# Two layers of attention and experts on one core: orders written by hand, set anew

## The chip, the cores and the metric

The kernel runs on one core of a Trainium2 chip, in float32. Its metric is the device time of one execution in microseconds (us). A core has five engines that run side by side, each through its own queue of instructions in order: TensorE (in the profile PE, with PEld for its weight loads), VectorE (DVE), ScalarE (ACT), GpSimd (POOL) and SyncE (SP), which here only starts DMA transfers. An engine waits on semaphores for the others. What is behind a waiting instruction in the same queue waits with it.

## The reference

```python
B, T, C = 4, 256, 1024                      # 1024 tokens of 1024 channels
x = x + lambda_layer(group_norm(x), ...)    # layer 0: q, k, v projections, content and position products
t = tokens(x)
t = t + attention(layer_norm(t), W_attn, b_attn, W_proj, b_proj)     # 16 heads, causal, 256 tokens
t = t + experts(layer_norm(t), gate_w, gate_b, expert_w, expert_b)   # 8 experts, kept where gate >= 0.1
```

The gate is a softmax over eight experts; weights below 0.1 are dropped and the rest are scaled to sum to one. Each expert is a 1024x1024 matrix.

## The kernel before

Tokens are worked on in eight tiles of 128 (`t`, `NT` = 8). Matrix products run in float32 as two passes, so a 128x128 by 128x512 product shows as two matmuls. Many products go by a scheme of seven block products instead of eight (`sums_of_A`, `sums_of_B` make the sums that it needs on VectorE). Accumulators lie in PSUM: three banks under the tag `mm`, three under `tr`, two under `sc`; a new user of a bank waits until the one three before it has been read out.

A list scheduler orders each engine's instructions by its own estimate of times, except within `tc.manual_schedule(...)`, where the engines named (all, if none is) keep the order in which the program is written. Two such sections that follow each other can still be merged: the first instructions of the later one can go ahead of the last of the earlier one.

**The end of layer 0 (L437 to L481).** Eight tiles, first the odd, then the even ones (`tiles`, position i). In each: `content` adds two products to `s0` (L375), two products `py` are added to the tile's rows in `x_at` (L477), and `layer_norm` (L183) takes statistics (L187 to L189), a square root on ScalarE (L132), and writes the normalised rows to one of three slots of `ln_rows` (L160). These rows are to be turned so that channels lie on the partitions: they go out to DRAM (L194), come back as four quarters (L173, `quarters_of`), and VectorE transposes 32x32 blocks of them into `ln1` (L178, `turn`). SyncE's order is the written one, that is, rows of tile i out, quarters of tile i in, rows of tile i+1 out; VectorE's order is the scheduler's. GpSimd adds a bias to the rows (L479) and stores them (L480). `project_v` then reads `ln1`: products 1 and 2 of the tiles in the order 1, 3, 0, 2, then product 3, then those that need `sums_of_B` (L507 to L510).

**Attention (L702 on).** 32 steps i, one pair of heads and one batch each. In step i VectorE turns the softmax rows of step i-3 (`turned`, L671), TensorE does some `project_qk` products (`units`), then `values` of step i-3 (L683), then `scores` of step i (L614); softmax follows on VectorE, ScalarE and GpSimd (`scored`), and its rows go out to DRAM and back on SyncE's queue (L662, L666). From step 22 on all engines keep the written order. From step 28 on, `project_out` of some token tile and half (t, j) stands in the step (`out_at`), its `values` after the seventh of its eight chunks. Half 0 uses `w_p0`, half 1 `w_p1`, which is loaded at step 28.

**Gating (L985 to L1110).** `project_out` of the remaining tiles is cut in chunks of one 128-row product (two matmuls). A counter `chunks` goes up by one per chunk, and the table `after` says at which count each of six stages of each tile's gate is written: 0 `normalise` (statistics, rows out, quarters in, residual rows to the output), 1 `turn_rows`, 2 `gate_sums` (L945), 3 `gate` (softmax, L953 to L972), 4 `place` (L979 to L1002), 5 `enter` (L1013). Tiles 6 and 7 are turned on TensorE (L931) from rows made on VectorE (L918). The first expert's two weight halves `w0` (2 MB each) and its bias are loaded on SyncE's queue ahead of this section.

**Experts (from L1275).** The last tile runs densely through expert 0 (`weighted`, L817), while its gate is finished; rows of the others are gathered by GpSimd (`get`, L802), transposed on VectorE (`put`, L178), multiplied (`products`, L1201) and added to the output by GpSimd (L825; the dense tile at L1296).

Of the kernel before, what the change touches and what calls it, by code (L numbers as in the profile page):

```python
# [32 lines left out]
F32 = mybir.dt.float32  # L33
# [6 lines left out]
P = 128  # L40
# [27 lines left out]
def kernel(  # L68
# [41 lines left out]
    def big_tile(n, name, shape=(NC, TOK)):  # L110
        return big[n].tile([P, *shape], F32, tag="big", name=name)

    def w_tile(name, *parts, home=None):

        w = (home or wpool).tile([P, NC, HALF], F32, tag="w", name=name)
        at = 0
        for part in parts:
            n = part.shape[1]
            nc.sync.dma_start(w[:, :, at : at + n], part.rearrange("(c p) n -> p c n", p=P))
            at += n  # L120
        return w

# [43 lines left out]
        )  # L166
        return done

    def quarters_of(rows, home, name):

        row = home.tile([P, Q, C // Q], F32, tag="xg", name=name)
        for f in range(Q):
            nc.sync.dma_start(row[ts(f, 32), :, :], rows[:, f, :].rearrange("(g j) c -> j g c", j=32))  # L173
        return row
# [5 lines left out]
            row[:, : slots // 32, :].rearrange("p g (c i) -> p g c i", c=NC),  # L180
        )

    def layer_norm(ln, t, dst, home, turns):  # L183

        stats = small.tile([P, 2, 6], F32, tag="ln_stats", name=f"ln1_stats{t}")
        for j in range(2):
            nc.vector.bn_stats(stats[:, j, :], xs[t][:, ts(j, HALF)])  # L187
        mv = small.tile([P, 2], F32, tag="ln_mv", name=f"ln1_mv{t}")
        nc.vector.bn_aggr(mv, stats)  # L189
        rstd = small.tile([P, 1], F32, tag="ln_rstd", name=f"ln1_rstd{t}")  # L190
        inverse_root(rstd, mv[:, 1:2], EPS)
        done = normalised(ln, xs[t], mv[:, 0:1], rstd)
        rows = turns.tile([P, Q, C // Q], F32, tag="rows", name=f"ln1_rows{t}")
        nc.sync.dma_start(rows.rearrange("n f c -> n (f c)"), ln)  # L194
        turn(dst[:, :, ts(t, P)], quarters_of(rows, home, f"ln1_quarters{t}"))
        return done


    with ExitStack() as layer0:
# [254 lines left out]
        turns = layer0.enter_context(tc.tile_pool(name="turns0", bufs=3, space=bass.MemoryType.DRAM))  # L454
        ln_rows = wpool.tile([P, 4, C], F32, tag="w", name="ln_rows")
        bp = ln_rows[:, 3, :]
        nc.gpsimd.dma_start(bp, b_proj.partition_broadcast(P))
        with tc.manual_schedule(engines={mybir.EngineType.SP}):
            for i, (b, nt) in enumerate(tiles):
                if i == 0:  # L460
                    content(b, nt)
                if i + 1 < NT:
                    content(*tiles[i + 1])
                t = 2 * b + nt
                for hp in range(2):
                    py = mm(f"py{t}_{hp}")
                    for hl in range(2):
                        bh = b * HEADS0 + 2 * hp + hl
                        for mh in range(2):
# [14 lines left out]
    with ExitStack() as attention:  # L484
# [41 lines left out]
        def project_v(r):  # L526
            a = [w_v[r][:, 4 * j : 4 * j + 4, ts(i, M)] for i in range(2) for j in range(2)]
            a11, a12, s3, a22 = a
            s1, s2, s4 = (s_v[:, r, i, :, :] for i in range(3))
            with tc.issue_after(ln_done.ins):  # L530
                sums_of_A(*a, s1, s2, s4)

            def one(t, n, a, b):
                return product(f"pv{r}_{t}_{n}", lambda c: b[:, c, ts(t, P)], lambda c: a[:, c, :], M)

            def homes(t):
                return [v1[2 * r + i][:, 4 * l + t, :] for i in range(2) for l in range(2)]

            in_time = (1, 3, 0, 2)
            for t in in_time:  # L540
                c11, c12, c21, c22 = homes(t)
                nc.scalar.copy(c22, one(t, 1, a11, b11))
                nc.vector.tensor_add(c11, one(t, 2, a12, b21), c22)
            if r == 0:
                sums_of_B()

            for t in in_time:
                nc.scalar.copy(homes(t)[1], one(t, 3, s4, b22))
            for t in range(4):
# [170 lines left out]
        for i in range(written):  # L720
# [8 lines left out]


        units = {
            22: ([(6, 4), (6, 5)], []),
            23: ([], [(7, 1)]),
            24: ([(7, 2)], [(7, 6)]),
            25: ([(7, 7), (7, 4)], []),
            26: ([(6, 3)], [(7, 5)]),
            27: ([(7, 3)], []),
        }
        out_at = {28: (0, 0), 29: (1, 0), 30: (0, 1), 31: (1, 1), 32: (2, 0), 33: (2, 1)}
        with tc.manual_schedule():  # L740
            for i in range(written, len(steps) + lag):
                if i == written:
# [43 lines left out]
    weights = ExitStack()  # L786
    w_even, t_pool = pool(weights, "w_even", 2), pool(weights, "t_pool")

    def half_weights(e, r, home, name="w_e"):

        return w_tile(f"{name}{e}_{r}", expert_w[e][:, ts(r, HALF)], home=home)
# [67 lines left out]
    with ExitStack() as gating:  # L859
# [40 lines left out]
        nc.vector.memset(kept, 0.0)  # L900
        kept_short = l2.tile([P, 2], F32, tag="kept_short", name="kept_short")

        def normalise(t):

            stats = small.tile([P, 2, 6], F32, tag="ln_stats", name=f"ln2_stats{t}")
            for j in range(2):
                nc.vector.bn_stats(stats[:, j, :], xs[t][:, ts(j, HALF)])  # L907
            mv = small.tile([P, 2], F32, tag="ln_mv", name=f"ln2_mv{t}")
            nc.vector.bn_aggr(mv, stats)
            rstd = small.tile([P, 1], F32, tag="ln_rstd", name=f"ln2_rstd{t}")  # L910
            inverse_root(rstd, mv[:, 1:2], EPS)
            row = l2w.tile([P, C], F32, tag="ye", name=f"row{t}", bufs=3)
            if t < NT - 2:
                normalised(row, xs[t], mv[:, 0:1], rstd)
                nc.sync.dma_start(rows[ts(t, P), :], row)
                row = quarters_of(rows[ts(t, P), :].rearrange("n (f c) -> n f c", f=Q), l2w, f"quarters{t}")
            else:
                nc.vector.tensor_scalar(row, xs[t], mv[:, 0:1], rstd, ALU.subtract, ALU.mult)  # L918
            nc.sync.dma_start(out[ts(t, P), :], xs[t])
            return row  # L920

# [132 lines left out]
                nc.vector.tensor_copy(slot[ts(g, 32), a:b, :, :], pc[ts(g, 32), a:b, :, g::Q])  # L1054
# [8 lines left out]
        def stage(n, t):  # L1063
# [24 lines left out]

        def one_more():
            nonlocal chunks  # L1090
            chunks += 1
            for t in after:
                for n, at in enumerate(after[t]):
                    if at == chunks:
                        stage(n, t)

        with tc.manual_schedule():
            for t in range(3, NT):
                for j in range(2):
# [34 lines left out]
        w, bias, step, T, T3, A, S = {0: w0}, {0: bias0}, {}, {}, {}, {}, {}  # L1134

        def load(e):
            w[e] = [half_weights(e, r, w_odd if e % 2 else w_even) for r in range(2)]
# [137 lines left out]
        with tc.manual_schedule():  # L1275
# [3 lines left out]
            for k in range(3):  # L1279
# [2 lines left out]
                lambda: gated[NT - 1][0][:, 0, 1:2],  # L1282
                turned_rows[NT - 1],
                w0,
                bias0,
                l2w,
                "dense",
                {
# [144 lines left out]
```

## Time and profile before

| what | value |
|---|---|
| runs shown | 1303.72, 1301.97, 1301.44 us |
| median | 1301.97 us |
| profiled execution: its own time | 1300.31 us |
| profiled execution: span from first to last instruction | 1298.5 us |
| mean granted TensorE clock | 0.984 |
| busy: PE, DVE, POOL, ACT | 1245.8, 709.9, 358.0, 214.7 us |

The profile comes from one execution. In a timeline a line has the start, the time, the engine, the source line, the operation with output<-input, the count, and in brackets the idle time of that engine before it and what ended it. "issue" is a wait that the profile can't ascribe. Busy time of TensorE is not time at full rate: after a long wait its instructions take about twice as long for some us.

### The profile page before, as it was taken

To read this page: it belongs to the slowest core of one execution; us is meant where nothing else is said; L and a number is where in the kernel's file an instruction comes from. 1 tells how busy PE (TensorE), PEld (TensorE's weight loads), DVE (VectorE), ACT (ScalarE), POOL (GpSimd) and SP (SyncE) were. 2 spreads that over 40 slices of the span, in tenths; PEclk is the share of its full clock that TensorE was granted. 3 is DMA by queue.
4 is the path that set the end of the run, shared out by engine and by line. 5 is a ranking of instruction groups with operands and counts; after the bars stand their busy time and mean duration, and the time that the engine had idled before them with its cause. 6 is when DMAs were issued, how large, how long until landed. Compare 5 with 4: busy or idle time off the path is not lost.

```text
span 1298.5 us, 12774 instructions
## 1 busy us (share of the span) xinstructions
PE 1245.8 (96%) x4562; PEld 650.9 (50%) x4562; DVE 709.9 (55%) x1303; ACT 214.7 (17%) x502; POOL 358.0 (28%) x439
## 2 busy tenths in 40 slices
PE   9999999978999999998988799899999999999998
PEld 5444894767884444443433344444344434443443
DVE  5884210686333666655544565756657464665642
ACT  3300111110000222222122223101111011011110
POOL 0000160250000222221221011543644554263530
PEclk9999999999999999998989899999999999999999
DMA  9020022854202535352377524455667475647442
GB/s 351 4 65 14 3 71 67 316 182 143 65 1 65 154 107 162 100 172 85 101 232 220 179 98 141 151 146 134 159 184 223 98 218 139 174 106 219 97 81 51
DMA packets 92823, 171.31 MB, mean 132 GB/s; under 512 B 9392, under 2 KB 47296, under 8 KB 92752
## 3 DMA queue, kind: packets, MB, share of 16 engines
q1 hardware_dynamic: 77616, 122.64, 28.7%
q0 software_dynamic: 15136, 47.78, 15.6%
q8 instruction: 38, 0.62, 0.2%
q14 instruction: 33, 0.27, 0.1%
HBM read 116.64 MB, written 49.55 MB: 128 GB/s over the span
## 4 chain that ended last, share of the span: by engine, by line
PE 42%; DVE 3%; issue 2%; DMA 2%; POOL 1%; ACT 1%; SPq 0%; DVEq 0%; POOLq 0%; ACTq 0%
PE p L1201 29%; PE po L701 6%; PE left L1243 3%; PE rest L1257 2%; PE last_pe L1358 1%; DMA w_p<-in_W_projT_dram 1%; DMA w_e_xg<-rows,gather 1%; POOL w_e_xg L802 1%; PE pqk L519 1%; PE pa L683 1%; DVE ln_stats L907 0%; DVE row_T L178 0%; PE sc L614 0%; PE parts L945 0%; POOL out_dram L1296 0%
## 5 line engine op out<-in xcount | busy, mean ns | idle before, releaser
L802 POOL DMA_INDIRECT w_e_xg<-rows,gather x146 | 155.1, 1062 | 61.5 <-issue 41.1
L1201 PE MATMUL p<-w_e,A 128*128 128x512 f32 x368 | 165.4, 600 | 1.6 <-DVE slot L1054 1.6
L656 POOL TENSOR_TENSOR s_q<-s_q,total 128x128 f32<-128x128 f32 (+1 forms) x128 | 64.4, 533 | 330.7 <-DVE total L653 330.7
L701 PE MATMUL po<-w_p,y_T 128*128 128x512 f32 x256 | 122.5, 619 | 5.8 <-DMA w_p<-in_W_projT_dram 5.8
L1201 PEld LDWEIGHTS p<-w_e,A 128*128 128x128 f32 x368 | 70.4, 192 | 91.6 <-issue 90.6
L1201 PE MATMUL p<-T,S 128*128 128x512 f32 x256 | 112.7, 592 | 0.0
L825 POOL DMA_INDIRECT out_dram<-y,add x32 | 57.4, 1794 | 178.1 <-ACT y L1207 116.7
L1207 ACT ACTIVATE y<-y,slot 128x512 f32<-128x512 f32 x64 | 46.0, 721 | 344.0 <-DVE y L1215 187.5
L284 PE MATMUL pq<-w_q,xn 128*128 128x512 f32 x224 | 99.6, 596 | 1.4 <-DVE q_s L288 1.1
L642 ACT ACTIVATE s_q<-s,top 128x256 f32<-128x256 f32 (+1 forms) x128 | 56.6, 443 | 194.7 <-issue 151.5
L519 PE MATMUL pqk<-ln,w_qk 128*128 128x512 f32 x192 | 86.9, 603 | 0.0
L1201 PEld LDWEIGHTS p<-T,S 128*128 128x128 f32 x256 | 48.6, 190 | 60.8 <-issue 60.5
L701 PEld LDWEIGHTS po<-w_p,y_T 128*128 128x128 f32 x256 | 46.9, 195 | 54.7 <-issue 46.7
L178 DVE STREAM_TRANSPOSE A<-w_e_xg 128x1024 f32<-128x1024 f32 x32 | 39.6, 1238 | 56.6 <-DMA w_e_xg<-rows,gather 56.6
L284 PEld LDWEIGHTS pq<-w_q,xn 128*128 128x128 f32 x224 | 41.8, 190 | 51.8 <-issue 47.3
L519 PEld LDWEIGHTS pqk<-ln,w_qk 128*128 128x128 f32 x192 | 36.5, 193 | 44.3 <-issue 43.4
L519 PE MATMUL pqk<-T,S_qk 128*128 128x512 f32 x128 | 58.4, 599 | 0.0
L1201 PE MATMUL p<-T,A 128*128 128x512 f32 x128 | 57.5, 592 | 0.0
L1201 PE MATMUL p<-w_e,S 128*128 128x512 f32 x128 | 57.5, 592 | 0.0
L519 PE MATMUL pv<-w_v,ln 128*128 128x256 f32 x192 | 45.7, 393 | 10.0 <-DVE ln L178 10.0
L519 PEld LDWEIGHTS pv<-w_v,ln 128*128 128x128 f32 x192 | 37.8, 198 | 16.2 <-issue 10.7
L1243 PE MATMUL left<-w_e,one 128*32 128x512 f32 x312 | 41.8, 593 | 0.0
(268 smaller groups left out, 1751.3 us busy)
## 6 DMA issues: line engine op xcount, KB each, us to landing
w_e<-in_expert_w_dram SPq DMA_DIRECT2D x16, 2048.0 KB, 12.4
s_rows<-s_q SPq DMA_DIRECT2D x32, 384.0 KB, 2.4
s_rows<-s_rows SPq DMA_DIRECT2D x128, 96.0 KB, 2.3
w_qk<-in_W_attnT_dram SPq DMA_DIRECT2D x8, 1024.0 KB, 6.1
xn<-in_xT_dram SPq DMA_DIRECT2D x8, 512.0 KB, 7.8
x_at<-in_x_dram SPq DMA_DIRECT2D x8, 512.0 KB, 7.4
w_v<-in_W_attnT_dram SPq DMA_DIRECT2D x2, 2048.0 KB, 12.6
ln_rows<-ln_rows SPq DMA_DIRECT2D x8, 512.0 KB, 4.6
```

The lines of the kernel that those rows point to most:

```text
L178: nc.vector.transpose(row_T[:, :, :slots].rearrange("p c (g j) -> p g c j", j=32), row[:, : slots // 32, :].rearrange("p g (c i) -> p g c ...
L284: nc.tensor.matmul(pq, xn[:, c, ts(t, P)], w_q[kc][:, c, :], start=(c == 0), stop=(c == NC - 1))
L519: nc.tensor.matmul(bank, stationary(c), moving(c), start=(c == 0), stop=(c == NC // 2 - 1))
L642: nc.scalar.activation(blocks(h, qt), s[:, h, cols].rearrange("p (b f i) -> p b f i", f=Q, i=32), AF.Exp, bias=top[:, qt, h : h + 1], accu ...
L656: nc.gpsimd.tensor_mul(blocks(h, qt), blocks(h, qt), total[:, qt, h : h + 1].unsqueeze(2).unsqueeze(3).to_broadcast([P, 1 + qt, Q, 32]),)
L701: nc.tensor.matmul(po, y_T[:, c, ts(t, P)], w_p[j][:, c, :], start=(c == 0), stop=(c == NC - 1))
L802: nc.gpsimd.indirect_dma_start(out=row[:, g, :], out_offset=None, in_=table[: (TOK - P) * Q, :] if e in SHORT else table, in_offset=bass.I ...
L825: nc.gpsimd.indirect_dma_start(out=out[: TOK - P, :] if e in SHORT else out, out_offset=bass.IndirectOffsetOnAxis(ap=add[:slots, e, k : k ...
L1201: nc.tensor.matmul(bank, a[:, c, :], b[:, c, :], start=(c == 0), stop=(c == NC // 2 - 1))
L1207: nc.scalar.mul(y[i][:, ts(j, HALF)], y[i][:, ts(j, HALF)], slot[:, e, 1, 2 * pair + i : 2 * pair + i + 1])
L1243: nc.tensor.matmul(bank[ts(i, 32), :], stationary, w[of][j][:, c, :], start=(c == 0), stop=(c == NC - 1))
L1257: nc.tensor.matmul(bank[ts(i, 64), :], A[e, last][:, i * (NC // 2) + c, :64], w[e][j][:, i * (NC // 2) + c, :], start=(c == 0), stop=(c == ...
```

## The change

In layer 0, `turn` is taken out of `layer_norm` and VectorE's order is the written one: the turn of the tile at position i-1 stands after the normalisation of the tile at position i, for positions 0 to 5. The last two turns stand after the first `sums_of_A` of `project_v`; the quarters of these two tiles land in slots of `ln_rows`. In attention, one product moves from step 22 to 23, and `out_at` has another order and a seventh entry, so that the gating section begins with the second half of tile 3. In gating, the table `after` is new; the first expert's weights and bias are written at chunks 14, 20 and 26, the weights on GpSimd's queue; two instructions that load a function table into ScalarE are added; half the statistics of the last tile are written earlier, its rows are made in two halves, and seven warming matmuls are left out. In the experts, the fourth gather stands ahead of the dense tile's addition to the output.

```diff
-    def w_tile(name, *parts, home=None):
+    def w_tile(name, *parts, home=None, queue=nc.sync):
...
-            nc.sync.dma_start(w[:, :, at : at + n], part.rearrange("(c p) n -> p c n", p=P))
+            queue.dma_start(w[:, :, at : at + n], part.rearrange("(c p) n -> p c n", p=P))
...
-    def layer_norm(ln, t, dst, home, turns):
+    def layer_norm(ln, t, quarters, turns):
...
-        turn(dst[:, :, ts(t, P)], quarters_of(rows, home, f"ln1_quarters{t}"))
+        quarters_of(rows, quarters)
...
+        def turn_ln(t):
+            turn(ln1[:, :, ts(t, P)], to_turn[t])
...
-        with tc.manual_schedule(engines={mybir.EngineType.SP}):
+        with tc.manual_schedule(engines={mybir.EngineType.SP, mybir.EngineType.DVE}):
...
-                ln_done = layer_norm(ln_rows[:, i % 3, :], t, ln1, tpool, turns)
+                if i < NT - 2:
+                    to_turn[t] = tpool.tile([P, Q, C // Q], F32, tag="xg", name=f"ln1_quarters{t}")
+                else:
+                    to_turn[t] = ln_rows[:, NT - 1 - i, :].rearrange("p (f c) -> p f c", f=Q)
+                ln_done = layer_norm(ln_rows[:, 2 if i == NT - 1 else i % 3, :], t, to_turn[t], turns)
+                if 0 < i < NT - 1:
+                    turn_ln(tiles[i - 1][0] * 2 + tiles[i - 1][1])
...
-            with tc.issue_after(ln_done.ins):
+            if r == 0:
+                with tc.manual_schedule(engines={mybir.EngineType.DVE}):
+                    with tc.issue_after(ln_done.ins):
+                        sums_of_A(*a, s1, s2, s4)
+                    for b, nt in tiles[-2:]:
+                        turn_ln(2 * b + nt)
+            else:
                 sums_of_A(*a, s1, s2, s4)
...
-            22: ([(6, 4), (6, 5)], []),
-            23: ([], [(7, 1)]),
+            22: ([(6, 4)], []),
+            23: ([(6, 5)], [(7, 1)]),
...
-        out_at = {28: (0, 0), 29: (1, 0), 30: (0, 1), 31: (1, 1), 32: (2, 0), 33: (2, 1)}
+        out_at = {28: (0, 0), 29: (1, 0), 30: (2, 0), 31: (0, 1), 32: (1, 1), 33: (2, 1), 34: (3, 0)}
...
+        def first_stats(t):
+            half_stats[t] = small.tile([P, 2, 6], F32, tag="ln_stats", name=f"ln2_stats{t}")
+            nc.vector.bn_stats(half_stats[t][:, 0, :], xs[t][:, :HALF])
...
-                nc.vector.tensor_scalar(row, xs[t], mv[:, 0:1], rstd, ALU.subtract, ALU.mult)
+                for j in range(2):
+                    half = slice(j * HALF, j * HALF + HALF)
+                    nc.vector.tensor_scalar(row[:, half], xs[t][:, half], mv[:, 0:1], rstd, ALU.subtract, ALU.mult)
...
-        w0 = [half_weights(0, r, w_even) for r in range(2)]
-        bias0 = expert_bias(0, l2w)
+        w0, bias0 = [], []
...
-            0: (1, 11, 13, 14, 19, 24),
-            1: (3, 20, 22, 23, 28, 33),
-            2: (12, 29, 31, 32, 37, 42),
-            3: (21, 38, 40, 41, 46, 51),
-            4: (33, 47, 49, 50, 55, 60),
-            5: (49, 59, 61, 62, 67, 72),
-            6: (65, 69, 71, 72, 76, 79),
+            0: (8, 13, 16, 17, 22, 27),
+            1: (8, 21, 24, 25, 30, 35),
+            2: (14, 29, 32, 33, 38, 43),
+            3: (22, 37, 40, 41, 46, 51),
+            4: (33, 45, 48, 49, 54, 59),
+            5: (49, 58, 61, 62, 67, 72),
+            6: (65, 69, 71, 72, 76, 80),
...
+        def load_table(function):
+            of = small.tile([P, 1], F32, tag="first", name="first", bufs=1)
+            nc.scalar.activation(of, ident[:, 0:1], function)
+        others = {
+            14: lambda: w0.append(half_weights(0, 0, w_even, queue=nc.gpsimd)),
+            20: lambda: w0.append(half_weights(0, 1, w_even, queue=nc.gpsimd)),
+            26: lambda: bias0.append(expert_bias(0, l2w)),
+            74: lambda: load_table(AF.Sqrt),
+            77: lambda: first_stats(NT - 1),
         }
...
+            chunks = NC - 1
+            one_more()
             for t in range(3, NT):
-                for j in range(2):
+                for j in range(t == 3, 2):
...
-            for _ in range(14):
+            for _ in range(7):
                 nc.tensor.matmul(warm[:, :P], before, ones, start=True, stop=True)
             stage(0, NT - 1)
+            load_table(AF.Exp)
...
+            get(0, 3)
             nc.gpsimd.indirect_dma_start(
...
-            get(0, 3)
             for e in range(E):
```

More of the change, by code (lines that the diff above doesn't have):

```diff
@@ L167, in normalised, with quarters_of @@
         return done
-    def quarters_of(rows, home, name):
-        row = home.tile([P, Q, C // Q], F32, tag="xg", name=name)
+    def quarters_of(rows, row):
         for f in range(Q):
@@ L456 @@
         bp = ln_rows[:, 3, :]
+        to_turn = {}
+        def turn_ln(t):
+            turn(ln1[:, :, ts(t, P)], to_turn[t])
         nc.gpsimd.dma_start(bp, b_proj.partition_broadcast(P))
-        with tc.manual_schedule(engines={mybir.EngineType.SP}):
+        with tc.manual_schedule(engines={mybir.EngineType.SP, mybir.EngineType.DVE}):
             for i, (b, nt) in enumerate(tiles):
@@ L787, with half_weights @@
     w_even, t_pool = pool(weights, "w_even", 2), pool(weights, "t_pool")
-    def half_weights(e, r, home, name="w_e"):
-        return w_tile(f"{name}{e}_{r}", expert_w[e][:, ts(r, HALF)], home=home)
+    def half_weights(e, r, home, name="w_e", queue=nc.sync):
+        return w_tile(f"{name}{e}_{r}", expert_w[e][:, ts(r, HALF)], home=home, queue=queue)
     def expert_bias(e, home, name="w_e", tag="bias", bufs=1):
@@ L901 @@
         kept_short = l2.tile([P, 2], F32, tag="kept_short", name="kept_short")
+        half_stats = {}
+        def first_stats(t):
+            half_stats[t] = small.tile([P, 2, 6], F32, tag="ln_stats", name=f"ln2_stats{t}")
+            nc.vector.bn_stats(half_stats[t][:, 0, :], xs[t][:, :HALF])
         def normalise(t):
-            stats = small.tile([P, 2, 6], F32, tag="ln_stats", name=f"ln2_stats{t}")
-            for j in range(2):
-                nc.vector.bn_stats(stats[:, j, :], xs[t][:, ts(j, HALF)])
+            if t not in half_stats:
+                first_stats(t)
+            stats = half_stats[t]
+            nc.vector.bn_stats(stats[:, 1, :], xs[t][:, HALF:])
             mv = small.tile([P, 2], F32, tag="ln_mv", name=f"ln2_mv{t}")
@@ L915, in normalise @@
                 nc.sync.dma_start(rows[ts(t, P), :], row)
-                row = quarters_of(rows[ts(t, P), :].rearrange("n (f c) -> n f c", f=Q), l2w, f"quarters{t}")
-            else:
-                nc.vector.tensor_scalar(row, xs[t], mv[:, 0:1], rstd, ALU.subtract, ALU.mult)
+                row = l2w.tile([P, Q, C // Q], F32, tag="xg", name=f"quarters{t}")
+                quarters_of(rows[ts(t, P), :].rearrange("n (f c) -> n f c", f=Q), row)
+            else:
+                for j in range(2):
+                    half = slice(j * HALF, j * HALF + HALF)
+                    nc.vector.tensor_scalar(row[:, half], xs[t][:, half], mv[:, 0:1], rstd, ALU.subtract, ALU.mult)
             nc.sync.dma_start(out[ts(t, P), :], xs[t])
@@ L1078 @@
         after = {
-            0: (1, 11, 13, 14, 19, 24),
-            1: (3, 20, 22, 23, 28, 33),
-            2: (12, 29, 31, 32, 37, 42),
-            3: (21, 38, 40, 41, 46, 51),
-            4: (33, 47, 49, 50, 55, 60),
-            5: (49, 59, 61, 62, 67, 72),
-            6: (65, 69, 71, 72, 76, 79),
+            0: (8, 13, 16, 17, 22, 27),
[5 more added lines that the diff above has]
+            6: (65, 69, 71, 72, 76, 80),
+        }
+        def load_table(function):
[7 more added lines that the diff above has]
+            77: lambda: first_stats(NT - 1),
         }
@@ L1095, in one_more @@
                         stage(n, t)
+            others.get(chunks, lambda: None)()
         with tc.manual_schedule():
+            chunks = NC - 1
+            one_more()
             for t in range(3, NT):
-                for j in range(2):
+                for j in range(t == 3, 2):
                     project_out(t, j, {c: one_more for c in range(NC)})
@@ L1133 @@
         w_odd, two = pool(pairs, "w_odd", 2, side="right"), pool(pairs, "two", 2, side="right")
-        w, bias, step, T, T3, A, S = {0: w0}, {0: bias0}, {}, {}, {}, {}, {}
+        w, bias, step, T, T3, A, S = {0: w0}, {0: bias0[0]}, {}, {}, {}, {}, {}
         def load(e):
@@ L1284 @@
                 w0,
-                bias0,
+                bias0[0],
                 l2w,
```

## The prediction

> **What bounds the kernel now.** I read the page first, then the waits of TensorE, then its timeline round each wait, then the queues behind them.
>
> ```profile
> span 1298.5 us, 12774 instructions
> PE 1245.8 (96%) x4562; PEld 650.9 (50%) x4562; DVE 709.9 (55%) x1303; ACT 214.7 (17%) x502; POOL 358.0 (28%) x439
> ```
>
> TensorE is busy for all but 52.7 us, so only those, and stretches where it works slowly, can be won. The waits of TensorE (releaser; total, times, longest) say where they lie:
>
> ```profile
> PE pv L519 <- DVE ln L178: 10.0, 2, 8.1
> PE pa L683 <- DVE s_T L671: 8.5, 3, 5.8
> PE parts L945 <- issue: 7.7, 1, 7.7
> PE po L701 <- DMA w_p<-in_W_projT_dram: 5.8, 1, 5.8
> PE pn L1123 <- DVE U L1213: 2.8, 1, 2.8
> PE parts L945 <- DVE row_T L178: 2.4, 4, 0.8
> PE p L1201 <- DVE slot L1054: 1.6, 1, 1.6
> ```
>
> Every one is touched. TensorE's timeline shows that a long wait costs twice:
>
> ```profile
> 278.06 7.07 PE L519 MATMUL pv<-w_v,ln 128*128 128x256 f32 x32
> 293.28 5.80 PE L519 MATMUL pv<-w_v,ln 128*128 128x256 f32 x16 [8.15 <-DVE ln L178]
> 300.91 3.69 PE L519 MATMUL pv<-w_v,ln 128*128 128x256 f32 x16 [1.83 <-DVE ln L178]
> 599.02 1.55 PE L683 MATMUL pa<-s_T,v 128*64 128x256 f32 x8 [5.76 <-DVE s_T L671]
> 662.99 7.85 PE L701 MATMUL po<-w_p,y_T 128*128 128x512 f32 x14 [5.79 <-DMA w_p<-in_W_projT_dram]
> 699.67 0.87 PE L683 MATMUL pa<-s_T,v 128*64 128x256 f32 x8 [1.67 <-DVE s_T L671]
> 719.64 1.08 PE L945 MATMUL parts<-row_T,gw 128*32 128x128 f32 x16 [7.74 <-issue]
> 846.06 5.88 PE L1201 MATMUL p<-w_e,A 128*128 128x512 f32 x8 [1.62 <-DVE slot L1054]
> ```
>
> Sixteen `pv` take 5.80 after 8.15 us of waiting, 3.69 after 1.83. From 846 on the chain of waits is TensorE alone to the last two products, so what is won earlier comes through to the end.
>
> **The change, part by part.** Times are those of the profiled execution.
>
> *Layer 0: turns in written order.* VectorE's timeline around the first turns:
>
> ```profile
> 242.42 0.16 DVE L159 SCALAR_TENSOR_TENSOR ln_less<-ln_mv,ln_rstd 128x1 f32<-128x1 f32 x1
> 255.43 1.25 DVE L178 STREAM_TRANSPOSE ln<-ln_quarters 128x1024 f32<-128x1024 f32 x1
> 289.31 1.23 DVE L178 STREAM_TRANSPOSE ln<-ln_quarters 128x1024 f32<-128x1024 f32 x1
> ```
>
> The scheduler turned too late: tile 3's quarters landed at 270.7, its turn came at 289.31, and the quarter buffer it held kept SyncE back. That goes. But the new place is early. Turn 0 follows position 1's normalisation, which ends at 242.6; its quarters landed at 251.8. VectorE now stands still for 9.2 us, and behind it are the adds that free TensorE's banks. After a turn VectorE needs four adds of 0.69, two statistics of 0.69, five small steps and ScalarE's root: 5.3 us to the next normalisation's end. From one such end to that tile's turn: 1.5 (ScalarE's rows), 4.6 (rows landing, median), 4.6 (quarters, first issue to last landing) and 1.2 for the turn. So two tiles take 1.5+4.6+4.6+1.2+5.3 = 17.2 us where TensorE's pace is 2x7.0. Chain of ends: position 2 at 258.4, 3 at 265.1, then 4 at 275.6, 5 at 282.3, 6 at 292.8; turn 5 ends 294.3, position 7 ends 298.2 (before: 283.5). Rows 6 land at 298.9, SyncE issues their quarters until 300.8, rows 7 land at 305.4, their quarters at 310.1, turn 7 ends at 311.4. Before it ended at 307.4, with TensorE waiting on the sums right behind it (0.76 us). So +4. Bounds: with the shortest landings of this stretch (3.6 and 4.4) turn 7 ends about 307.5, +0; with long ones (5.2 and 5.3) about 317.5, +10. I take the medians.
>
> TensorE waits about 4 us twice in that loop; rows show no slowing after 1.83 and slowing after 5.76, nothing between. [...]
>
> The next weight half is loaded when `ln_rows` is free, now after turn 7 (311) and not at 303.4. Its first user starts at 340, its sums at 317 with 3.6 us to spare; 0 to +2, I take 0.
>
> *Product (6,5) from step 22 to 23.* Before, step 23's `values` had nothing in front and waited 5.76 for a turn written behind `sums_qk` on VectorE; with slow products after it, 584.47 to 610.46 took 26.0 us. New: TensorE reaches the end of step 22 at 589.7 and of (6,5) at 593.2. VectorE: mask 0.96 and maxima 1.0 to 591.9, sums 2.7 to 594.6, reciprocal and turn to 595.7. Wait 2.5, too short for slowing. Work 17.45 + 2.5 = 19.95: -6.0 (bounds -6.5, -3 if it slows).
>
> *Steps 28 to 34.* `w_p1` landed at 662.95; TensorE wanted it at 657. With (2,0) in between it is wanted 8.7 us later, at 665.7: a margin of 2.7. Turn 28 is the tightest: quarters landed 669.9, wanted turned at 671.9. Step 34 gets work before its `values`, so the 1.67 goes. TensorE's work alone from 656.08 to the eighth chunk adds up to 698.0, against 707.5: -9.5 (bound -6).
>
> *Gating.* The 7.74 is SyncE's queue:
>
> ```profile
> 701.15 0.40 SPq L119 DMA_DIRECT2D w_e<-in_expert_w_dram  x1
> 701.63 0.74 SPq L795 DMA_DIRECT2D w_e_bias<-in_expert_b_dram  x1
> 702.43 1.80 SPq L915 DMA_DIRECT2D rows<-row  x1
> ```
>
> Tile 0's rows were normalised at 687.3, were issued at 702.43 behind a weight half that waited for memory, and landed at 713.8 behind 4 MB. Without these three ahead they go at once. Tiles 0 to 2 are complete 7 to 22 us before their chunks; the wait goes with about 1.5 of slowing. Three chunks instead of two between turn and `gate_sums` remove 2.4, the list waits (1.02, 0.64, 0.33) go. GpSimd pays two issues at about 0.9 each (the gate weights' issue in as many pieces took 0.91), with nothing waiting behind. At the end of the section the root's table load (1.28), one statistic (0.6) and half a scaling (0.4) leave the path; the warming products were not on it.
>
> Against this stands one new wait. At chunk 49 the table now names tile 4's softmax ahead of tile 5's normalisation, both at 49; before, the softmax came at 50. It holds VectorE for 2.8 to 3.8 us (744.71 to 747.51, 722.99 to 726.76). Tile 5's rows had no slack: turned at 776.97, wanted at 777.18. So about 3.5 us of new wait before its `gate_sums`; with smaller ones in a denser VectorE I take 6. Net -(7.74+1.5+2.4+2.0+2.3)+6 = -10 (bounds -15, -6).
>
> ScalarE's rows show 1.28 for a table load and the next instruction 0.01 us later. [...]
>
> *Expert 0.* The fourth gather stood behind the output add, which waited until 830.74; VectorE then stood 4.56 us for it, with the bank readers behind. Now its four issues (1.26 each) start when turn 0 frees a buffer at 821.8, end at 828 and leave the add its time. VectorE is at the list copies' end by 842.0 instead of 846.16, TensorE goes on at 842.3 instead of 846.06, without the slow products (5.88 for eight against 3.6): -6.0; the earlier exponential table takes 0.4. I take -5.8 (bound -3).
>
> Sum: 4 - 6.0 - 9.5 - 10 - 5.8 = -27.3. From the profiled 1300.31: 1273.0. The median stands 1.66 above that execution: **1275**.
>
> **Rivals.** *Slower:* layer 0's in-order turns eat it all. Price by the same chain: 8 tiles at the loop's longest landings (7.84 and 5.56) put turn 7 at 331, +24, total 1295; it decides against the change from a round trip of 16 us on (+36, 1307). For it: the first round trip took 13.4. Against: that one ran beside 6 MB of loads; the later ones took 8 to 10. Chance 0.11. *Between:* that chain at 1290 to 1300, 0.06.
>
> *Weights start early.* The chunk numbers order GpSimd's queue but delay nothing, and the first half's memory is free once (7,3) is done, at 638. `w_p0` shows such a start: 559.63, for a step that began at 584. Then 2 MB (8.0 us alone) run beside `w_p1` and the softmax rows: up to 5 us of wait for `w_p1`, +1 to 2 slow: 1282. Chance 0.18.
>
> *All cover holds:* quiet landings in layer 0 (+0), no new gating wait: 1265. Chance 0.17. *No effect* would need layer 0 to lose just what the rest wins: 0.03 for within 0.2%, about what a measurement here can tell from no change. Forecast: 0.45.
>
> **Numbers.** The likeliest is 1275. Far ends of the terms: 0-6.5-9.5-15-6.5 gives 1264; +10-3-6-6-3 gives 1294, and part of the slower-leaning cases adds 2. Faster 0.86, same 0.03, slower 0.11.
>
> **What would show it.** Right: in layer 0 waits of about 4 us on VectorE's adds in the loop and turn 7 near 311; `w_p` and `issue` gone from TensorE's waits; `parts` waiting 3 to 5 us once, for tile 5; `pn` gone. Wrong: turn 7 beyond 320 (layer 0), or a wait on `w_p` at 665 (early weights).

## The result, and the profile after

The kernel after takes 1284.93 us (median of four runs, 1284.55 to 1286.41) against 1302.85 for the kernel before, run beside it (1301.44 to 1303.81): ratio 0.9865, 95% interval 0.9848 to 0.9883. The forecast was 1275. The profiled execution took 1284.55, its span is 15.8 us shorter than that of before. The page:

```profile
span 1282.7 us, 12735 instructions
...
PE 1238.7 (97%) x4548; PEld 646.4 (50%) x4548; DVE 707.5 (55%) x1305; ACT 212.9 (17%) x502; POOL 361.9 (28%) x441
```

TensorE now stands idle for 44.0 us (1282.7 less 1238.7) instead of 52.7, and its own time fell by 7.1: seven warming products are gone, and fewer products follow a long wait (the mean granted clock is 0.992 instead of 0.984). Its waits (total, times, longest):

```profile
PE parts L972 <- issue: 11.8, 1, 11.8
PE pv L530 <- DVE s_v L152: 3.9, 1, 3.9
PE parts L972 <- DVE row_T L177: 3.2, 1, 3.2
PE pa L700 <- DVE s_T L688: 3.2, 2, 2.1
PE pc L366 <- DVE s L374: 3.1, 2, 2.1
PE py L474 <- DVE s L374: 2.2, 1, 2.2
```

`w_p`, `pn` and `ln` are gone from this view. The `issue` wait, which was to go, has grown from 7.7 to 11.8. TensorE's timeline at the places that the prediction named:

```profile
595.07 0.95 PE L700 MATMUL pa<-s_T,v 128*64 128x256 f32 x8 [2.08 <-DVE s_T L688]
...
597.53 7.92 PE L530 MATMUL pqk<-ln,w_qk 128*128 128x512 f32 x16
...
766.71 1.08 PE L972 MATMUL parts<-row_T,gw 128*32 128x128 f32 x16 [3.25 <-DVE row_T L177]
...
831.97 3.67 PE L1244 MATMUL p<-w_e,A 128*128 128x512 f32 x8 [1.32 <-DVE slot L1081]
```

Step 23 waits 2.08, tile 5's gate sums 3.25, and the products behind the list copies (`slot`) only 1.32. What stands behind the 11.8 is seen where all engines are listed together, from the last `values` product on:

```profile
692.15 1.24 ACT L160 ACTIVATE row<-xb,ln_less,ln_rstd 128x1024 f32<-128x1024 f32 x1 [18.45 <-PE pa L700]
...
693.41 0.34 SPq L939 DMA_DIRECT2D rows<-row  x1
...
694.25 0.93 POOL L119 DMA_DIRECT2D w_e<-in_expert_w_dram  x1
...
695.41 0.90 POOL L119 DMA_DIRECT2D w_e<-in_expert_w_dram  x1
...
696.65 1.93 SPq L172 DMA_DIRECT2D quarters<-rows  x4
...
711.83 1.08 PE L972 MATMUL parts<-row_T,gw 128*32 128x128 f32 x16 [11.81 <-issue]
...
714.14 1.74 SPq L172 DMA_DIRECT2D quarters<-rows  x4
```

ScalarE could write tile 0's row only at 692.15, after standing 18.45 us; its wait ended with the last `values`. SyncE sent the row at 693.41 and asked for the quarters at 696.65. In between GpSimd issued both weight halves, at 694.25 and 695.41, and the quarters landed at 704.32 to 710.36, 13.7 us from the first issue to the last landing; those of tile 3, later and with no weights beside them, took 4.4 (728.33 to 732.68). Tile 1's row, issued at 699.15, landed at 714.12.

By the prediction's own terms, from the two traces:

| term | predicted | traces |
|---|---|---|
| layer 0 | +4 | 65.6 (246.66 to 312.26) to 65.8 (246.01 to 311.79): +0.2 here; +2.5 alone (run below) |
| step 22 to 23 | -6.0 | 26.0 to 21.4: -4.6 |
| steps 28 to 34 | -9.5 | 51.45 to 41.9: -9.5 |
| gating, to the dense products | -10 | 98.7 to 102.1: +3.4 |
| expert 0 | -5.8 | 39.9 to 37.0, and 8 products 5.9 to 3.7: -5.1 |
| sum | -27.3 | -15.6 |

### The profile page after: what moved, and what is told of

Its sections match the earlier page's. It is cut to its first block, busy times and chain, and to the rows that moved or that the text cites. A ratio compares the mean times of both kernels' runs of the same rounds, so it can differ in the third digit from the quotient of the medians.

```text
span 1282.7 us, 12735 instructions
## 1 busy us (share of the span) xinstructions
PE 1238.7 (97%) x4548; PEld 646.4 (50%) x4548; DVE 707.5 (55%) x1305; ACT 212.9 (17%) x502; POOL 361.9 (28%) x441
## 2 busy tenths in 40 slices
DMA packets 91799, 171.31 MB, mean 134 GB/s; under 512 B 9392, under 2 KB 47296, under 8 KB 91728
## 4 chain that ended last, share of the span: by engine, by line
PE 44%; DVE 3%; DMA 2%; ACT 1%; issue 1%; POOL 1%; SPq 0%; DVEq 0%; ACTq 0%; POOLq 0%
PE p L1244 30%; PE po L718 6%; PE left L1286 3%; PE rest L1300 2%; DMA quarters<-rows 1%; PE last_pe L1401 1%; DMA w_e_xg<-rows,gather 1%; PE pa L700 1%; PE pqk L530 1%; POOL w_e_xg L819 1%; DMA rows<-row 0%; PE sc L631 0%; ACT L989 0%; DVE row_T L177 0%; PE parts L972 0%
## 5 line engine op out<-in xcount | busy, mean ns | idle before, releaser
L819 POOL DMA_INDIRECT w_e_xg<-rows,gather x146 | 158.2, 1084 | 58.8 <-issue 39.9
L177 DVE STREAM_TRANSPOSE A<-w_e_xg 128x1024 f32<-128x1024 f32 x32 | 39.6, 1239 | 52.7 <-DMA w_e_xg<-rows,gather 52.7
L490 POOL TENSOR_TENSOR x_at<-x_at,ln_rows 128x1024 f32<-128x1024 f32 x8 | 19.3, 2407 | 76.6 <-ACT ln_rows L160 76.6
## 6 DMA issues: line engine op xcount, KB each, us to landing
w_e<-in_expert_w_dram SPq DMA_DIRECT2D x14, 2048.0 KB, 11.7
```

The costliest lines, as they stand in the source:

```text
L177: nc.vector.transpose(row_T[:, :, :slots].rearrange("p c (g j) -> p g c j", j=32), row[:, : slots // 32, :].rearrange("p g (c i) -> p g c ...
L819: nc.gpsimd.indirect_dma_start(out=row[:, g, :], out_offset=None, in_=table[: (TOK - P) * Q, :] if e in SHORT else table, in_offset=bass.I ...
```

## The experiments

Ratios are to the kernel before, run beside each kernel on the same chip. Two theories to begin with: T, the first expert's transfers beside tile 0's quarters make the 11.8; M, the row's memory alone makes it. In every fence below a timeline line has start, time, engine, line, operation and the idle time before it.

**The weights later.**

```diff
-            14: ... half_weights(0, 0, w_even, queue=nc.gpsimd)
-            20: ... half_weights(0, 1, w_even, queue=nc.gpsimd)
+            23: ... half_weights(0, 0, w_even, queue=nc.gpsimd)
+            31: ... half_weights(0, 1, w_even, queue=nc.gpsimd)
```

> The kernel after, with the first expert's two weight halves at chunks 23 and 31 of the table instead of 14 and 20, so that on GpSimd's queue they stand behind tile 0's and tile 1's list products, which wait for VectorE. Theory T (the 11.8 us before tile 0's gate sums are tile 0's quarters, stretched by 4 MB of weights that GpSimd issued at 694 and 695): the quarters land in 3 to 5 us again, the turn ends near 702, the wait falls from 11.8 to 2 or 3 us and takes the slow products after it along; later rows share the rings with the weights, which can give up to 3 us back: 1274 to 1278 us. Rival M (tile 0's row is held by memory until the last values product, and that alone sets the wait): the wait stays at 10 us or more, 1284 to 1286 us.

1283.51 us, ratio 0.9863 (0.9849 to 0.9877). The quarters landed within 4.2 us of their first issue, the wait fell from 11.8 to 2.2: T's mechanism holds, M's does not. But T's time is missed. The halves went out at 716.4 and 728.1; tile 3's row, issued at 718.8, took 8.1 us and its quarters up to 8.3. VectorE waited for them until 737.80, its list work stood behind, and TensorE waited there:

```profile
739.19 1.08 PE L972 MATMUL parts<-row_T,gw 128*32 128x128 f32 x16 [3.52 <-DVE place L1012]
```

The stretch from the last `values` to the dense products is 99.8 us, 3.1 less than in the kernel after; the rest turned up at later tiles.

**The bias tile first.** Only the allocation of the tile moves, ahead of the rows:

```diff
         w0, bias0 = [], []
+        bias_home = l2w.tile([P, Q, C // Q], F32, tag="bias", ...)
...
-            26: lambda: bias0.append(expert_bias(0, l2w)),
+            26: lambda: (nc.sync.dma_start(bias_home, ...), bias0.append(bias_home)),
```

> The kernel after, with the tile for the first expert's bias allocated ahead of the rows, as the kernel before had it; its load stays at chunk 26 and the weights at chunks 14 and 20. Tile 0's row then lies where it lay before and should be written near 686 or earlier instead of 692. Theory T: tile 0 comes through ahead of the weights, but tile 1's rows, issued near 699, land behind 4 MB near 713, are turned near 720 and TensorE stands about 9 us there instead: 1282 to 1286 us. Rival M: the wait is gone and nothing takes its place: 1273 to 1276 us.

1283.0 us, ratio 0.9859 (0.9844 to 0.9874). The row was written at 677.7 and its quarters had landed at 689.9, so this alone takes tile 0's wait away; then tile 1's row, issued at 701.6 beside the weights, landed at 710.2, its quarters at 715.6, and TensorE stood 6.16 us, until 717.14, behind that. T foresaw the place and the time, with 9 us for 6.2.

**Both.**

> The kernel after with both edits, weights at chunks 23 and 31 and the bias tile allocated first. Theory T: like the weights alone, less the 2 to 3 us that were left of the wait: 1272 to 1276 us, no wait over 1 us before tile 0's gate sums. Rival M: the same time as with the bias tile alone, within 1 us.

1283.01 us, ratio 0.9859 (0.9843 to 0.9875): nothing before tile 0's gate sums, but 5.47 before tile 3's at 737.49. T's time is missed again, for the same reason as in the first run. Moved as whole halves, the weights only choose which tile pays: the ratios of the three runs, 0.9863, 0.9859 and 0.9859, can't be told from the 0.9865 of the kernel after.

**Layer 0's part alone**, put into the kernel before.

> The kernel before with layer 0's part of the change alone (the turns of the first normalisation in written order on VectorE, the last two tiles' quarters in the row buffers, the sums of A ahead of the last two turns). The prediction's term: +4 us (0 to +10), 1303 to 1313 us, likeliest 1307. What the trace of after shows: the last turn ends at 306.9 instead of the worked-out 311.4 and the first product with T starts 0.5 us earlier than before, so 1301 to 1304 us, no change. The prediction's slower rival: +24 us, 1327.

1302.81 against 1300.94 us: ratio 1.0019 (1.0010 to 1.0028), by which it is +2.5 us (1.3 to 3.6). The prediction's sign stands, at two thirds of its size, and what I read from the trace of after alone was wrong. The first product with T starts at 314.5 here. In ten traces with this layer 0 it starts between 311.8 and 315.0, 313.7 in the mean; the profiled execution of after is the earliest of them. In the two with the old layer 0 it starts at 312.3 and 311.7.

**The kernel after again.**

> The kernel after itself, beside the other variants on one chip, as what they are compared with. The profiled execution of after reached its first product with T at 311.8 us, four other kernels with the same layer 0 at 314.2 to 314.6. If that is chance between executions, this one stands near 314 there too and the median is 1.3 to 1.5 per cent under the kernel before; if it belongs to the kernel, it stands at 312 again.

1285.07 us, ratio 0.9878 (0.9862 to 0.9894). 312.4 this time, the same 11.78 us before tile 0's gate sums, 102.5 us for the gating section. What differs between executions is layer 0; the gating section is the same.

**Weights in the gaps.** Four pieces of 1 MB, each behind a copy of one element per partition from a tile's quarters; the bias tile first; tile 5's normalisation at chunk 48.

```diff
-            14: ...  20: ...
+            nc.gpsimd.tensor_copy(behind, normal[t][:, 0, :1])
+            nc.gpsimd.dma_start(w0[r][:, 4 * k : 4 * k + 4, :], ...)
+            29: piece(0, 0, 2), 37: piece(0, 1, 3), 45: piece(1, 0, 4), 58: piece(1, 1, 5)
-            5: (49, 58, ...
+            5: (48, 58, ...
```

> The kernel after with the bias tile allocated first, the first expert's 4 MB loaded in four pieces of 1 MB, each held on GpSimd's queue by a small copy from the quarters of tiles 2, 3, 4 and 5, so that it starts when a tile's quarters have landed and not beside them, and tile 5's normalisation one chunk earlier, ahead of tile 4's softmax on VectorE. Theory T (the waits of the gating section are the weights' transfers beside one tile's rows, plus the normalisation behind the softmax): no wait over 1.5 us is left before any gate sums; of 102.1 us between the end of the eighth chunk and the dense products 11.8 + 3.25 and some 2 us of slow products go: 13 to 16 us under the kernel after. Rival C (what is taken from one tile turns up at the next, because VectorE's order and SyncE's queue are full): another wait of 4 us or more stands at a later tile and the gain over the kernel after is 2 to 5 us.

1280.59 us, ratio 0.9841 (0.9826 to 0.9856). No wait before any gate sums, but a new one. VectorE's timeline:

```profile
741.51 0.16 DVE L159 SCALAR_TENSOR_TENSOR ln_less<-ln_mv,ln_rstd 128x1 f32<-128x1 f32 x1
751.23 0.69 DVE L720 TENSOR_TENSOR xb<-xb,po 128x512 f32<-128x512 f32 x1 [9.56 <-DMA out_dram<-xb]
```

At chunk 48 the table comes ahead of the last addition to tile 5's rows. The row was normalised, and the tile's rows stored, without it, so that this kernel leaves half of that projection out of tile 5; the addition then waited 9.56 us for the store; tile 4's softmax and TensorE's `pp` (9.67 at 754.86, ten slow products after it) waited behind. The fault lies in the order that I gave; the run says nothing for C, and its time decides nothing between C and T.

**The same, softmax behind.** Tile 5 back at 49, tile 4's softmax at 50.

```diff
-            4: (33, 45, 48, 49, 54, 59),
-            5: (48, 58, 61, 62, 67, 72),
+            4: (33, 45, 48, 50, 54, 59),
+            5: (49, 58, 61, 62, 67, 72),
```

> The kernel after with the bias tile allocated first and the first expert's 4 MB in four pieces held behind the quarters of tiles 2 to 5, as in the run before it; tile 5's normalisation is back at chunk 49, and tile 4's softmax goes from chunk 49 to 50, behind it (in the run before, tile 5 was normalised at chunk 48, ahead of the last half of its output projection, so its row lacked that half, and the late addition then waited for the store of the row). Theory T (the transfers beside one tile's rows and VectorE's order are all that makes TensorE wait in this section): no wait over 2 us before any gate sums, softmax or placement; the 102.5 us between the last values product and the dense products fall to 83 to 87, 15 to 19 us under the kernel after, 1266 to 1270 us. Rival C (what one tile is given, a later one pays): a wait of 4 us or more at a later tile, 92 us or more, 1274 to 1280 us.

1268.69 us, ratio 0.9729 (0.9716 to 0.9743). The stretches from the last `values` to the dense products, in the view by windows (time, then busy time and count of PE, PEld, DVE, ACT, POOL, then granted clock, DMA share, GB/s), of the kernel after:

```profile
692.10:794.99 102.89, 84.53 (x444) 40.72 (x444) 61.21 (x247) 28.05 (x38) 11.35 (x21) 0.93 0.47 161
```

and the kernel with gaps and the softmax behind:

```profile
693.50:778.89 85.39, 81.36 (x444) 39.16 (x444) 60.47 (x247) 26.71 (x36) 13.56 (x27) 1.00 0.53 173
```

102.9 us became 85.4, as T has it, and no wait over 1.7 us is left in the section. 18.4 us in which TensorE stood became 4.0, and the same 444 matmuls took 3.2 us less, with the granted clock at 1.00 instead of 0.93. Both kernels move 171.31 MB in all; what differs is when the weights go, where the bias tile lies and the softmax's chunk. The bias tile alone had brought no time. To the softmax's place belong the 3.25 us before tile 5's gate sums and the slow products behind them; no run moves it alone.

**Turns two positions behind in layer 0**, with a third quarter buffer.

```diff
-                if 0 < i < NT - 1:
-                    turn_ln(tiles[i - 1][0] * 2 + tiles[i - 1][1])
+                if 1 < i:
+                    turn_ln(tiles[i - 2][0] * 2 + tiles[i - 2][1])
```

> The kernel after with layer 0's turns two positions behind the normalisation instead of one (three quarter buffers instead of two). Theory T (the written order makes VectorE wait out each round trip through DRAM, so the loop runs at half a round trip per tile): the three waits in the loop (2.1, 1.0, 2.2 us) and the 3.9 us before the products with the sums of A go, the loop keeps 7.0 us a tile, the last turn ends near 298 instead of 307 to 309, the first product with T starts near 306: 6 to 10 us under the kernel after. Rival: at the faster pace rows and quarters land later (4.6 us each as in the kernel before), SyncE's queue becomes the chain, and the gain is 0 to 3 us.

1283.35 us, ratio 0.9865 (0.9849 to 0.9882). The loop's waits went, but the first product with T starts at 310.8, not 306. On all engines' timeline:

```profile
290.74 3.39 POOL L490 TENSOR_TENSOR x_at<-x_at,ln_rows 128x1024 f32<-128x1024 f32 x1 [6.33 <-ACT ln_rows L160]
291.97 3.25 DVE L152 TENSOR_TENSOR s_v<-w_v,s_v 128x1024 f32<-128x1024 f32 x1
...
297.65 2.90 PE L530 MATMUL pv<-w_v,ln 128*128 128x256 f32 x6 [7.49 <-DVE ln L177]
```

The rival named SyncE's queue; that was not it. The tile of position 5 had its quarters by 283.0, but the sums of A (289.25 to 296.35) went ahead of its turn at 296.27, and TensorE stood 7.49 for it. Of the 6 to 10 us expected that left 1.7 in the medians.

**Product (7,1) ahead in step 23 too.**

```diff
-            23: ([(6, 5)], [(7, 1)]),
+            23: ([(6, 5), (7, 1)], []),
```

> The kernel after with product (7,1) ahead of step 23's values as well, and nothing behind them. Theory (the 2.08 us wait costs itself and 1.5 us of slow products after it): the product waits at most 1.4 us for its sums, the slow products go, 2 to 3.5 us under the kernel after. Rival: the softmax of step 23 starts 3.6 us later and its turn is late at step 26: no gain, 0 to +2 us.

1283.44 us, ratio 0.9868 (0.9851 to 0.9885). From step 22's product to step 25's values, 33.6 us (584.63 to 618.20) in the kernel after again became 31.0 (586.06 to 617.03): -2.6, inside the expectation. The 2.08 us and the slow products went; one wait of 1.11 came, at 604.88. The medians differ by 1.6, less than was expected, and the two profiled executions by 1.3; of the latter layer 0 hides 1.4, by which it was slower in this one.

**The three that help together**, with the turns of positions 5 and 6 ahead of the sums.

> The kernel of the run above, with product (7,1) ahead in step 23 (measured 2.6 us in that stretch of the trace) and layer 0's turns two positions behind, this time with the turns of positions 5 and 6 ahead of the sums of A on VectorE (in the run with the lag alone, the sums took 6.9 us ahead of position 5's turn, whose quarters had landed 13 us before, and TensorE stood 7.49 us for it). Theory: the first product with T starts at 304 to 306 us instead of 312 to 314.5, and all three parts add: 9 to 12 us under the run above, 1255 to 1260 us. Rival: the last tile's round trip (normalised near 289, turned near 300) sets the start of T's products whatever VectorE's order: the first product with T at 309 or later, 4 to 6 us under the run above.

1263.52 us, ratio 0.9694 (0.9681 to 0.9706): the fastest of all, 5.2 under the run with the gaps. The size is the rival's, the cause neither's. The first product with T starts at 309.9, and the last tile's turn had ended at 302.3; TensorE had stood 5.45 us until 300.13 for the sums of A, which now came late, and the 32 products behind that wait took 9.96 instead of 7.07. VectorE has the turns and the sums to do at the same place, and either order leaves one of them late.

**The fourth gather behind the add again.**

```diff
-            get(0, 3)
             nc.gpsimd.indirect_dma_start(    # the output add
...
+            get(0, 3)
```

> The kernel after with the fourth gather put back behind the output add on GpSimd's queue. Prediction's step: the gather ahead of the add is worth most of 5.8 us (VectorE stood 4.56 us for it in the kernel before): 3.5 to 6 us slower than the kernel after, the wait for the slot of the lists or the gather back before expert 0's products. Rival: in the kernel after the output add no longer waits as long (the section before it ends earlier on every queue), so the place matters by under 1.5 us.

1292.3 us, ratio 0.9915 (0.9902 to 0.9928), 0.37% over the kernel after again: some 5 us. The wait is back where the kernel before had it:

```profile
836.00 0.59 PE L1166 MATMUL pn<-kept_short,ones 128*128 128x2 f32 x2 [3.27 <-DVE U L1256]
```

From the dense products to those behind the list copies it is 40.3 us instead of 36.7, and these eight took 5.48 instead of 3.67: 5.4.

**The steps' part alone**, put into the kernel before.

> The kernel before with the attention steps' part alone: product (6,5) in step 23, the output projections reordered with tile 3's first half in step 34, and the gating table's first eight chunks counted off ahead of the rest. Prediction's terms: 6.0 and 9.5, 15.5 us together; by the trace of after, 4.6 and 9.5, 14.1 us: 1286 to 1288 us. Rival: the gating section gives part back, since tile 0's rows stand on SyncE's queue behind a weight half that waits for memory and then lie beside 4 MB, and TensorE has eight chunks less to do meanwhile: the wait before the gate sums grows from 7.7 to over 12 us and the gain is 8 to 10 us.

1292.24 us, ratio 0.9914 (0.9902 to 0.9927): -11.2 us. All engines' timeline after the steps:

```profile
678.53 13.27 SPq L119 DMA_DIRECT2D w_e<-in_expert_w_dram  x2
...
692.48 0.42 SPq L915 DMA_DIRECT2D rows<-row  x1
...
709.92 1.08 PE L945 MATMUL parts<-row_T,gw 128*32 128x128 f32 x16 [13.78 <-DVE row_T L178]
```

This is the rival's mechanism at somewhat less than its price: the last `values` ended 9.7 us earlier than before, the second weight half still stood on SyncE's queue until its memory was free (the two halves' line lasts 13.27 us), and the wait grew from 7.7 to 13.8. By this trace the steps took 15.7 us less (26.0 to 19.8 and 51.45 to 41.9) and the gating section 7.1 more (98.7 to 105.8). The steps are worth 15 us only where the gating section does not give part of it back.

## Why the prediction held in direction and missed by 10 us

**Steps 28 to 34** and **expert 0** are right, in size and in cause: the wait for `w_p` and the 1.67 of step 34 are gone, and putting the gather back costs about what the prediction gave for it (5.4 in the trace, some 5 in the medians, against 5.8).

**Step 22 to 23.** The wait was worked out as 2.5 and measured 2.08. The step that failed is "too short for slowing", which was my estimate: no row showed it for a wait of 2.5, and after the 2.08 the scores took 1.65 instead of 0.92 and sixteen products 7.92 instead of 7.13, 1.5 us in all. The prediction found no row between waits of 1.83 and 5.76; the last line of its first timeline is one, since the eight products in 5.88 us stand behind waits of 2.84 and 1.62. In the run of the steps alone the same 2.08 us were followed by products at their rate and the stretch took 19.8 us, -6.2, as predicted. Between these two traces what differs is when the wait falls (below), and the prediction did not ask for that, so where the term comes true it is by luck.

**Layer 0.** +4, and +2.5 (1.3 to 3.6) alone. The chain was of the right form: VectorE waits out round trips between the normalisations. Its links were shorter. Rows landed 3.1 us after their issue in the median instead of the 4.6 taken from the kernel before; why is not shown (in the two kernels whose turns lag by two it was 3.5 and 3.9). So the ends of the chain came 2.4 to 5.5 us early each, TensorE's waits in the loop were 1.0 to 2.2 instead of 4 (up to 3.6 in other profiles of this layer 0), and the last turn ended at 306.9 in the profile of after and at 309.7 in that of layer 0 alone, against 311.4.

**Gating** carries the whole miss: it is off by 13.4 us, the sum by 11.7, the other terms give 1.7 back. That they give any back is chance: with layer 0 at the +2.5 of its own run instead of +0.2 they would add 0.6 to the miss. Two steps failed.

"Without these three ahead they go at once" took the row to be ready when its statistics are. Tile 0's row needs memory too. The bias tile used to be the first of its pool; with its allocation moved to chunk 26 the row takes its place, and that place came free only with the last `values`. The run with the bias tile first shows it: 677.7 instead of 692.15. So the chain hung on the last `values`, which the steps' part brings forward: from their end to the first gate sums passed 19.1 us before and 19.1 with the steps alone (there by way of the weight half that waited for memory) and 19.7 after, while the work of TensorE in between shrank from 11.4 to 7.9 with tile 3's first half gone from it. A gain ahead of such a chain turns into a wait behind it. I had counted it in both places.

The second is that chunks 14 and 20 were taken for a delay. The rival "weights start early" said that they only order GpSimd's queue, and it was right, but it had the collision at 638, beside `w_p1`. GpSimd's queue stood behind the clearing of the gate weights, which also waited for the last `values` (18.00 us, until 692.17). So 4 MB went out at 694, beside exactly the rows that TensorE needed next. Where both are put right, in the run with the softmax behind, the section takes 84.6 us instead of 98.7: -14.1, near the 15.9 of gains that the prediction had added up before the new wait.

The new wait for tile 5 was worked out well, and it went when the softmax stood behind the normalisation: 3.5 predicted, 3.25 measured, with 1.09 and 1.00 as the smaller ones.

## What to carry to other kernels

A step in a written table is only an order; whatever must start late has to wait for something that happens late, and a copy of one element per partition from the data that must land first was enough here. When work is taken from in front of a wait, look for what the wait hangs on before counting the gain: if that is the end of the same stretch, the gain comes back as waiting. And the time at which a tile is first allocated decides whose memory it inherits, so moving an allocation alone moved an instruction by 14.5 us here.

## What the runs showed of the hardware

**Slow products after short waits.** The length of a wait does not decide alone. After 1.67 and 1.83 us TensorE kept its rate in the kernel before, and after 1.71 in the run with the weights in the gaps; in the run with the weights later, four products took 3.37 instead of 1.96 after 1.67. After the 2.08 of step 23 sixteen products took 7.92 in the kernel after, 8.03 in the same kernel again and 8.40 after the 2.09 of the run with both edits (7.13 otherwise); in the steps alone 7.13. After 2.24 to 2.53 sixteen `py` took 5.23 to 5.53 (3.71 otherwise), after 2.17 4.05; after 2.79 four `pc` took 1.98, in another kernel after 2.81 they took 3.78. The granted clock, third from the end in these lines, tells more. First the kernel after, then the steps alone, round the same wait:

```profile
592.33:595.74 3.41, 1.33 (x10) 0.49 (x8) 3.34 (x7) 0.43 (x2) 1.51 (x4) 1.00 0.44 115
595.74:599.15 3.41, 3.41 (x14) 2.01 (x11) 2.44 (x5) 0.01 (x1) 0.39 (x1) 0.50 0.29 115
```

```profile
589.89:593.30 3.41, 3.01 (x8) 0.99 (x6) 3.31 (x7) 1.86 (x8) 0.16 (x1) 1.00 0.29 115
593.30:596.71 3.41, 1.73 (x17) 1.24 (x17) 3.29 (x7) 0.00 (x0) 1.90 (x4) 1.00 0.45 115
```

In the profiles of the kernels before and after, but for the tail of each, the clock stands at half for 3.41, 6.83 or 10.24 us at a time, that is 3.41 once, twice or three times, and the times at full clock between two of these are whole multiples of 3.41 too (from 14 of them, 47.79 us, to 150, 512.00 us), so that the changes mark off stretches of that length. In the kernel after the wait lies whole in one of them (TensorE busy for 1.33 us of 3.41), and the next runs at half clock. In the steps alone an edge at 593.30 (counted on in such stretches from the half clock that began at 289.52) divides it, 1.73 us of the second stretch are busy, and the clock stays. In the two profiles every stretch at full clock with 2.08 us or more of idle time has one at half clock behind it, eleven in all, and none with 1.85 us or less has; between the two figures there is none. Behind the waits of 2.08 to 2.53 us named above stood 0 to 2 us of slow work.

**VectorE and GpSimd took longer beside each other, but only in some operations.** The sum L152, 1.21 us alone, took 3.03 in the kernel after and 3.25 in the run with the turns two behind while GpSimd added 1024 elements per partition, and GpSimd's 2.35 became 2.79 and 3.39: VectorE lost 1.8 and 2.0 us, GpSimd 0.4 and 1.0, and both times L152 ended 1.09 us after GpSimd's addition. Where the two did not overlap, in the fastest kernel, both had their usual 1.22 and 2.35. Transposes (1.23 to 1.25), statistics (0.69) and the additions from PSUM (0.67) ran beside the same GpSimd work unchanged. Size did not decide it: in the kernel before, L159, which works out one element per partition, took 2.12 us instead of 0.16 beside such an addition and ended with it, at 283.5. Why some operations are slowed and others not is not shown.
